# Sums over states by accumulating transfers, C in two banks, and unsplit MLP inputs in a hybrid attention and state-space kernel

## The chip, the cores and the metric

The kernel runs on one core of one Trainium2 chip. A core has five engines with a queue each: TensorE (PE in the profile; its weight loads are PEld), VectorE (DVE), ScalarE (ACT), GpSimd (POOL) and SyncE (SP), which issues most transfers. Sixteen DMA engines carry out the transfers of all queues. Data lie in SBUF, in PSUM (eight banks of 128 x 512 fp32, where PE writes) or in DRAM. The metric is the device time of one execution in microseconds (us); smaller is better.

## The reference

The input x has 4 sequences of 1024 tokens with 128 channels, fp32. Four residual blocks follow one another, each on a LayerNorm of x: attention (16 heads, a window of 32 keys and every 64th key), an MLP, a state-space block, and the same MLP again.

```python
x = x + attn(layernorm(x))
x = x + ffn(layernorm(x))
x = x + mamba(layernorm(x))     # mamba itself adds its input: out = inp + res_scale * ...
x = x + ffn(layernorm(x))

# ffn: three products with weights of +1 and -1, 128 -> 512 -> 512 -> 128, relu between
h = relu(s0 * (concat[x, -x] @ w0)) * 2
h = relu(s1 * (h @ w1)) * 2
return s2 * (h @ w2)

# mamba, E = 256 channels, N = 16 states, per sequence; the core of it:
def step(h, inp):
    dt_t, B_t, C_t, u_t = inp
    dA = exp(dt_t[..., None] * A)
    h = dA * h + (dt_t * u_t)[..., None] * B_t[:, None, :]
    y_t = einsum('ben,bn->be', h, C_t)          # the sum over the 16 states
    return h, y_t
y = (ys + u2 * D_param) * silu(z)
out = y @ W_out
```

## The kernel before

**Stages.** Attention fills the first 232 us. Then comes a stage of MLPs and preparation (232 to 319 us), then the scans of the state-space block (319 to 866 us), with the remaining MLPs of both kinds woven in between, then an end of 35 us.

**Units of the scan.** A half batch is one sequence and one half of its 1024 tokens; there are 8, in the order of `parts_in_order`. A unit is one half batch and one of the 16 states, so there are 128 (`units`). Channels lie on the partitions, in two halves h of 128 (`NH` = 2), tokens run along the free axis (`CH` = 512). For unit i the function `scans` (line 1134; its main loop is at 1211) issues:

- `load_b` (1142): every second unit, a transfer on SP's queue that brings two rows of B, copied to all partitions (`bs`, 512 KB, two buffers);
- `drive` (1150), two units ahead: POOL multiplies `du` by `bs` into `db` (128 x 1024, three buffers);
- `decay` (1158), one unit ahead: ACT takes the exponential into a PSUM bank (`da`, two banks), one h at a time;
- a product on PE that spreads C's row over the partitions into PSUM (`pcc`, one bank);
- two scans on DVE, one for each h, from `da` and `db` into `hs`; the last column is kept in `carry` for the second half of the sequence;
- one product on DVE, `hs` by `pcc`, into `hc` (128 x 1024, six buffers);
- `fold` (1164): POOL adds the `hc` of an even unit to that of the next odd unit, one h in each unit;
- `total` (1171): PE adds the folded pair into `pys` (a PSUM bank for each h), as an fp32 product with the identity. A half batch starts with the product for the term u2 * D (`skip_d`) and has eight such sums for each h;
- `gated` (1183): after the eighth, DVE multiplies the gate by `pys`.

Of the eight PSUM banks, five belong to the scans (`da` 2, `pcc` 1, `pys` 2), three to all other work (`SPARE`, line 1252).

**The order of the work.** Every instruction of the scans goes out through one helper (line 57), and each engine's order is the program's. The other work (MLPs, LayerNorms, preparation of later half batches) is written as generators that yield pieces with estimated costs. `pieces` (1295) is called twice in each unit and issues those that fit by the planner's clock of each engine (`times`, advanced by `spend`, 1256) and by a rate per call (`RATES`, 1278); `evictions` (1282) issues those that empty a PSUM bank. What is left when the last unit is out is issued after it. So the estimates decide at which unit a piece stands in an engine's queue; they do not decide when it runs.

**The MLP** (`mlp`, 739) takes 512 tokens (256 in the last pieces). Its steps: LayerNorm on ACT, four transposes on PE (`ftp`), the copy to SBUF (`fxnT`), the first product (`pf`), relu, the second (`pg`), relu, the third (`pfo`), the residual on DVE. All calls pass `split` as true: inputs of the first two products are held as two single-pass numbers, the rounded value (written by ACT) and the rest (written by DVE, in `empty`, 751), and PE multiplies both parts in turn. In the profile `a` names the MLPs of the first kind, `b` and `c` those of the second; `early`, `late` and `late_batch` (835 to 863) call `mlp`. `in_scan_buffers` (1334) lends buffers of the scan to one MLP that runs before the scans.

Of the kernel before, what the change touches and what calls it, by code (L numbers as in the profile page):

```python
# [43 lines left out]
def hybrid_kernel(ctx: ExitStack, tc: tile.TileContext, x, Wq, Wk, Wv, Wo, ln_g, ln_b, W_in, conv_w,  # L44
# [694 lines left out]
    def mlp(u, tiles, split, pool, lane, own=None, soon=False, hasty=False, stats=None):  # L739
# [39 lines left out]
        xnT = pool.tile([P, 2, cols], kind, name=f"fxnT{u}", tag=f"fxnT{lane}")  # L779
        yield from empty([xnT], [tp], False)  # L780
        for f0 in (0, 2):
            yield fill(1.1 if split else 1.8, 2, ready=(lambda: own or h1_free[0]) if f0 == 0 else None, loose=f0 == 2)
# [9 lines left out]
            for f in range(2):  # L792
                w = wt(w0[:, (f0 + f) * P : (f0 + f + 1) * P])
                for s in range(parts):
                    te.matmul(pf[f], w, xnT[:, s], start=s == 0, stop=s == parts - 1)
# [39 lines left out]
    def early(bp, c, *args):  # L835
        stats = yield from awaited(("a", bp, c))
        tiles = xs[bp][:, 4 * c : 4 * c + 4, :]
        yield from mlp(f"a{bp}_{c}", tiles, True, *args, hasty=bp == 1 and c < HALF, stats=stats)
        fed.add(("a", bp, c))
# [11 lines left out]
    def late_batch(b, f, groups, *args):  # L851
# [5 lines left out]
        yield from mlp(f"c{b}_{f}{groups[0]}", tiles, True, *args, soon=bool(f), stats=stats)  # L857
# [276 lines left out]
    def scans(wide, ready):  # L1134
# [3 lines left out]
        bss, dbs, das, hss = {}, {}, {}, {}  # L1138
# [10 lines left out]

        def drive(i):  # L1150
            if i <= last:
                b, f, n = units[i]
                ready(b, f, NH - 1)
                dbs[i] = m2.tile([P, NH, CH], F32, name=f"db{i}", tag="db", bufs=3)
                bs = bss[i - n % 2][:, n % 2]
                gp.tensor_tensor(dbs[i], mamba_pre[b, f][3], bs.unsqueeze(1).to_broadcast([P, NH, CH]), ALU.mult)
# [7 lines left out]
        def fold(i):  # L1164

            h = i % 2
            k = i - 2 - h
            if 0 <= k <= last:
                gp.tensor_add(hss[k + 1][:, h], hss[k + 1][:, h], hss[k][:, h])

        def total(i):

            h = 1 - i % 2
            k = i - 3 - h
            if not 0 <= k <= last:
                return
            b, f, n = units[k]
            if n == 0:
                py[b, f, h] = wide.tile([P, CH], F32, name=f"pys{b}_{f}{h}", tag=f"pys{h}")
                te.matmul(py[b, f, h], skip_d[:, h], mamba_pre[b, f][1][:, h], start=True, stop=False)  # L1180
            te.matmul(py[b, f, h], ident, hss[k + 1][:, h], start=False, stop=n == N - 2)

        def gated(i):

            h = i % 2
            k = i - 4 - h
            if not 0 <= k <= last:
                return False
            b, f, n = units[k]
            if n == N - 2:  # L1190
                gate = mamba_pre[b, f][0]
                ve.tensor_mul(gate[:, h], gate[:, h], py.pop((b, f, h)))
                if h == NH - 1:
                    fed.add(("g", b, f))
            return n == N - 2
# [12 lines left out]
        for h in range(NH):  # L1208
            decay(0, h)
            done["da", 0, h] = spend("sc", 0.7)  # L1210
        for i, (b, f, n) in enumerate(units):
            now[0] = i
            load_b(i + 3)
            fold(i)
            h0, h1 = i % 2, 1 - i % 2
            done["fold", i] = spend("gp", 1.29, *after(("hc", i - 1 - h0)))
            drive(i + 2)
            done["db", i + 2] = spend("gp", 2.38, *after(("hs", i - 1, 1)))
            pc = wide.tile([P, CH], F32, name=f"pcc{i}", tag="pcc")
            te.matmul(pc, spread[: 6 * N, n, :], mamba_pre[b, f][4], start=True, stop=True)  # L1220
            done["pcc", i] = spend("pe", 0.4, *after(("hc", i - 1)))
            hs = m2.tile([P, NH, CH], F32, name=f"hs{i}", tag="hs")
# [219 lines left out]
```

## Time and profile before

| what | us |
|---|---|
| median of the three runs | 908.13 |
| lowest and highest | 905.29, 908.22 |
| span of the profiled execution (the page gives no other time of it) | 901.9 |
| attention | 0 to 232 |
| MLPs and preparation | 232 to 318.75 |
| scans, first scan to the end of the last `hc` product | 318.75 to 866.45 |
| end | 866.45 to 901.9 |
| busy in the scans: PE, DVE, ACT, POOL | 472.1, 504.6, 409.3, 508.8 |

A group's line in the profile gives the source line (57 for nearly all, the helper), the engine, the operation, output <- inputs with shapes, and the count; then the busy time in us and the mean of one in ns; then the idle time of the engine just before these instructions and what ended it. A line of waits gives who waited for whom, the time in total, how often, and the longest. A line of the timeline gives start, duration, engine, operation and how many instructions it merges; one fp32 product of PE appears as two. In the busy table by stretches each engine's column is us busy, with the number of its instructions in brackets; the last columns are PE's granted clock, the mean busy share of the 16 DMA engines and the rate that they moved.

### The profile page before, as it was taken

How to read it: one execution, taken by the hardware profiler on the slowest of the kernel's cores; microseconds unless marked ns; L12 is line 12 of the kernel's file. 1: busy time of each engine (PE TensorE's matmuls, PEld its weight loads, DVE VectorE, ACT ScalarE, POOL GpSimd, SP SyncE). 2: the span in 40 equal slices, each digit the busy share in tenths (PEclk: the TensorE clock that was granted, in tenths of full speed). 3: DMA queues.
4: the chain of work that ended last, by engine and by line, in shares of the span. 5: the costliest groups of instructions: out<-in, count | busy, mean ns of one | idle time of the engine just before them, and what ended most of it. 6: DMA issues, size and time to landing. Idle time of an engine off the chain costs nothing. (4 is left out here: it accounts for less than half of the span.)

```text
span 901.9 us, 16464 instructions
## 1 busy us (share of the span) xinstructions
PE 756.2 (84%) x6226; PEld 463.5 (51%) x6226; DVE 754.3 (84%) x994; ACT 607.1 (67%) x1358; POOL 727.0 (81%) x566
## 2 busy tenths in 40 slices
PE   5897779866798978879899888779889989989777
PEld 2454546544577642335456554335455545656457
DVE  6799999999533289798899999989988898999962
ACT  4776648744445488888787888888777766654423
POOL 6799958998322199999999999999988987997930
PEclk9899989987789997789999999899989999999899
DMA  4733123330100111121221211212111121221100
GB/s 127 131 73 70 43 44 69 72 65 2 43 7 1 49 53 66 67 74 48 70 69 51 70 48 70 72 47 72 70 72 59 53 78 59 70 82 58 60 7 19
DMA packets 47152, 53.18 MB, mean 59 GB/s; under 512 B 4808, under 2 KB 38384, under 8 KB 47072
## 3 DMA queue, kind: packets, MB, share of 16 engines
q1 hardware_dynamic: 45904, 51.59, 20.4%
q8 instruction: 49, 0.80, 0.4%
q0 software_dynamic: 608, 0.27, 0.2%
q10 hardware_dynamic: 560, 0.26, 0.1%
q14 instruction: 31, 0.25, 0.1%
HBM read 45.82 MB, written 4.46 MB: 56 GB/s over the span
## 5 line engine op out<-in xcount | busy, mean ns | idle before, releaser
L57 POOL TENSOR_TENSOR db<-du,bs 128x1024 f32<-128x1024 f32 x128 | 302.4, 2363 | 0.1
L57 ACT ACTIVATE da<-dt,a_t 128x512 f32<-128x512 f32 x256 | 175.5, 688 | 123.2 <-DVE hs L57 122.7
L57 POOL TENSOR_TENSOR hc<-hc,hc 128x512 f32<-128x512 f32 x128 | 162.8, 1272 | 29.1 <-DVE hc L57 28.8
L57 DVE TENSOR_TENSOR hc<-hs,pcc 128x1024 f32<-128x1024 f32 x128 | 155.9, 1218 | 23.7 <-PE pcc L57 15.4
L57 DVE TENSOR_TENSOR_SCAN hs<-da,db 128x512 f32<-128x512 f32 x128 | 149.4, 1207 | 20.7 <-ACT da L57 15.5
L57 DVE TENSOR_TENSOR_SCAN hs<-da,carry,db 128x512 f32<-128x512 f32 x128 | 156.9, 1266 | 1.2 <-ACT da L57 1.2
L57 PE MATMUL pys<-hc,ident 128*128 128x512 f32 x256 | 145.3, 651 | 6.1 <-POOL hc L57 6.0
L57 POOL TENSOR_TENSOR prodv<-vS,E 128x128 f32<-128x128 f32 (+14 forms) x30 | 69.3, 2311 | 11.5 <-ACT E L57 11.3
L57 PEld LDWEIGHTS pys<-hc,ident 128*128 128x128 f32 x256 | 49.8, 208 | 53.7 <-issue 28.1
L57 PE MATMUL pcc<-bc,spread 96*128 96x512 bf16 x128 | 51.5, 402 | 29.6 <-DVE hc L57 28.7
L57 PE MATMUL pga<-h1a,w 128*128 128x512 f32 x256 | 70.5, 425 | 2.7 <-DVE h1a L57 1.9
L57 POOL TENSOR_TENSOR prod<-kv,qs 128x128 f32<-128x128 f32 (+14 forms) x30 | 71.1, 2369 | 0.8 <-DVE or L57 0.8
L57 ACT ACT_TABLE_LOAD x48 | 61.6, 1283 | 3.5 <-issue 2.6
L57 PE MATMUL pc<-mxnT,w_conv 128*128 128x512 f32 x128 | 61.5, 606 | 2.0 <-ACT gate L57 2.0
L57 PEld LDWEIGHTS pga<-h1a,w 128*128 128x128 f32 x256 | 49.3, 195 | 25.5 <-issue 4.7
L57 ACT ACTIVATE E<-S 128x512 f32<-128x512 f32 (+15 forms) x62 | 26.5, 473 | 39.7 <-DVE S L57 39.5
L57 PE MATMUL ps<-kx,qT 64*32 64x256 f32 x1008 | 43.5, 416 | 5.8 <-DVE S L57 5.0
L57 POOL TENSOR_TENSOR du<-dt,u 128x512 f32<-128x512 f32 x16 | 20.4, 1275 | 30.5 <-ACT dt L57 30.5
L57 ACT COPY ep<-pt 128x512 f32<-128x512 f32 x32 | 18.7, 586 | 35.8 <-DVE eo L57 35.5
L57 PEld LDWEIGHTS pc<-mxnT,w_conv 128*128 128x128 f32 x128 | 24.6, 194 | 33.9 <-issue 26.7
L57 PE MATMUL pgb<-h1b,w 128*128 128x512 f32 x128 | 37.5, 439 | 4.8 <-DVE h1b L57 3.3
L57 PE MATMUL pgc<-h1c,w 128*128 128x256 f32 (+1 forms) x192 | 37.2, 346 | 0.0
(244 smaller groups left out, 1637.5 us busy)
## 6 DMA issues: line engine op xcount, KB each, us to landing
bs<-bd SPq DMA_DIRECT2D x64, 512.0 KB
vr<-vd SPq DMA_DIRECT2D x32, 256.0 KB
vd<-kv SPq DMA_DIRECT2D x8, 256.0 KB
x<-in_L_attn_a_x_dram SPq DMA_DIRECT2D x15, 128.0 KB
kx<-kT SPq DMA_DIRECT2D x104, 16.0 KB
out_dram<-x SPq DMA_DIRECT2D x8, 128.0 KB
taps<-in_L_attn_b_conv_w_dram SPq DMA_DIRECT2D x1, 512.0 KB
out_dram<-ox SPq DMA_DIRECT2D x2, 256.0 KB
```

The costliest lines, as they stand in the source:

```text
L57: ins = getattr(self.engine, name)(*args, **kwargs)
```

## The change

1. The product `hs` by `pcc` is written back over the unit's `db`. Two units share one tile (1 MB, `[P, 2, NH, CH]`). The tile of a half batch's first pair (`acc`, two buffers) collects: for pairs two to seven POOL issues a transfer that adds the pair's tile to it (`gather`). The tiles of pairs two to eight come from three buffers (`pr`). The folds on POOL are gone.
2. PE adds the eighth pair, and then the collecting tile, in the first units of the next half batch: for each h the `skip_d` product and four sums, h after h in one bank (`pys`). After the last unit they follow at once, with h = 1 in a bank of `pcc`.
3. `pcc` has two banks, and the spread of unit i + 1 is issued in unit i.
4. The MLP's input `fxnT` is one fp32 copy by ACT, multiplied by PE in one fp32 product. It stays split in the first two MLPs (buffers lent from `gate`) and in the last two half MLPs.
5. The planner's figures follow (`spend`, `fill`).

```diff
--- before.py
+++ after.py
@@ -736,7 +736,7 @@
 
     h1_free = [True]
 
-    def mlp(u, tiles, split, pool, lane, own=None, soon=False, hasty=False, stats=None):
+    def mlp(u, tiles, split, pool, lane, own=None, soon=False, hasty=False, stats=None, halves=None):
 
 
 
@@ -776,10 +776,15 @@
         tp = bank(f"ftp{u}")[:, :cols]
         for i in range(nt):
             te.transpose(tp[:, i * P : (i + 1) * P], xn[:, i, :], ident)
-        xnT = pool.tile([P, 2, cols], kind, name=f"fxnT{u}", tag=f"fxnT{lane}")
-        yield from empty([xnT], [tp], False)
+        if halves:
+            xnT = halves(u)
+            yield from empty([xnT], [tp], False)
+        else:
+            xnT = pool.tile([P, 1, cols], F32, name=f"fxnT{u}", tag=f"fxnT{lane}")
+            yield evict(sc=0.57)
+            sc.copy(xnT[:, 0], tp)
         for f0 in (0, 2):
-            yield fill(1.1 if split else 1.8, 2, ready=(lambda: own or h1_free[0]) if f0 == 0 else None, loose=f0 == 2)
+            yield fill(1.1 if halves else 2.1, 2, ready=(lambda: own or h1_free[0]) if f0 == 0 else None, loose=f0 == 2)
             if f0 == 0:
                 if own:
                     h1 = own(u)
@@ -790,9 +795,11 @@
                 h2 = pool.tile([P, 4, cols], F32, name=f"h2{u}", tag=f"h2{lane}")
             pf = [bank(f"pf{u}_{f0 + f}")[:, :cols] for f in range(2)]
             for f in range(2):
-                w = wt(w0[:, (f0 + f) * P : (f0 + f + 1) * P])
-                for s in range(parts):
-                    te.matmul(pf[f], w, xnT[:, s], start=s == 0, stop=s == parts - 1)
+                w = w0[:, (f0 + f) * P : (f0 + f + 1) * P]
+                w = w if halves else w.bitcast(F32)
+                n = xnT.shape[1]
+                for s in range(n):
+                    te.matmul(pf[f], w, xnT[:, s], start=s == 0, stop=s == n - 1)
             yield from empty(h1[f0 : f0 + 2], pf, True)
         for f0 in (0, 2):
             yield fill(2.05 if split else 1.8, 2, loose=f0 == 2)
@@ -835,7 +842,8 @@
     def early(bp, c, *args):
         stats = yield from awaited(("a", bp, c))
         tiles = xs[bp][:, 4 * c : 4 * c + 4, :]
-        yield from mlp(f"a{bp}_{c}", tiles, True, *args, hasty=bp == 1 and c < HALF, stats=stats)
+        first = first_in if bp == 0 and c < HALF else None
+        yield from mlp(f"a{bp}_{c}", tiles, True, *args, hasty=bp == 1 and c < HALF, stats=stats, halves=first)
         fed.add(("a", bp, c))
 
     def late(bp, c, *args):
@@ -848,13 +856,13 @@
                 tiles[b2 * R : (b2 + 1) * R],
             )
 
-    def late_batch(b, f, groups, *args):
+    def late_batch(b, f, groups, *args, **kwargs):
 
         stats = yield from awaited(("c", b, f))
         g = slice(groups[0], groups[-1] + 1)
         tiles = own_x[b, f][:, g]
         stats = stats[:, :, g]
-        yield from mlp(f"c{b}_{f}{groups[0]}", tiles, True, *args, soon=bool(f), stats=stats)
+        yield from mlp(f"c{b}_{f}{groups[0]}", tiles, True, *args, soon=bool(f), stats=stats, **kwargs)
         to = out[b, f * (T // 2) : (f + 1) * (T // 2)].rearrange("(g p) c -> p g c", p=P)
         nc.sync.dma_start(to[:, g], tiles)
         fed.add(("b", b, f, groups[0]))
@@ -1135,7 +1143,7 @@
 
 
 
-        bss, dbs, das, hss = {}, {}, {}, {}
+        bss, prs, das, pcs = {}, {}, {}, {}
         py = {}
         last = len(units) - 1
 
@@ -1147,13 +1155,18 @@
                 bss[i] = m2.tile([P, 2, CH], F32, name=f"bs{i}", tag="bs", bufs=2)
                 nc.sync.dma_start(bss[i], mamba_pre[b, f][5][n : n + 2, :].partition_broadcast(P))
 
+        def pair(i):
+            return prs[i - i % 2][:, i % 2]
+
         def drive(i):
             if i <= last:
                 b, f, n = units[i]
                 ready(b, f, NH - 1)
-                dbs[i] = m2.tile([P, NH, CH], F32, name=f"db{i}", tag="db", bufs=3)
+                if n % 2 == 0:
+                    tag, bufs = ("pr", 3) if n else ("acc", 2)
+                    prs[i] = m2.tile([P, 2, NH, CH], F32, name=f"pr{i}", tag=tag, bufs=bufs)
                 bs = bss[i - n % 2][:, n % 2]
-                gp.tensor_tensor(dbs[i], mamba_pre[b, f][3], bs.unsqueeze(1).to_broadcast([P, NH, CH]), ALU.mult)
+                gp.tensor_tensor(pair(i), mamba_pre[b, f][3], bs.unsqueeze(1).to_broadcast([P, NH, CH]), ALU.mult)
 
         def decay(i, h):
             if i <= last:
@@ -1161,38 +1174,42 @@
                 das[i, h] = wide.tile([P, CH], F32, name=f"da{i}_{h}", tag="da", bufs=2)
                 sc.activation(das[i, h], mamba_pre[b, f][2][:, h], AF.Exp, scale=a_t[:, h, n : n + 1])
 
-        def fold(i):
-
-            h = i % 2
-            k = i - 2 - h
-            if 0 <= k <= last:
-                gp.tensor_add(hss[k + 1][:, h], hss[k + 1][:, h], hss[k][:, h])
-
-        def total(i):
-
-            h = 1 - i % 2
-            k = i - 3 - h
-            if not 0 <= k <= last:
-                return
-            b, f, n = units[k]
-            if n == 0:
-                py[b, f, h] = wide.tile([P, CH], F32, name=f"pys{b}_{f}{h}", tag=f"pys{h}")
+        def spread_c(i):
+            if i <= last:
+                b, f, n = units[i]
+                pcs[i] = wide.tile([P, CH], F32, name=f"pcc{i}", tag="pcc", bufs=2)
+                te.matmul(pcs[i], spread[: 6 * N, n, :], mamba_pre[b, f][4], start=True, stop=True)
+
+        def gather(i):
+
+            k = i - 2
+            if not 0 <= k <= last or k % 2 or units[k][2] in (0, N - 2):
+                return False
+            gp.dma_start(prs[k - units[k][2]], prs[k], accum_op=ALU.add)
+            return True
+
+        def total(e, h, step, tag="pys"):
+
+            b, f, n = units[e]
+            if step == 0:
+                py[b, f, h] = wide.tile([P, CH], F32, name=f"pys{b}_{f}{h}", tag=tag, bufs=2 if tag == "pcc" else 1)
                 te.matmul(py[b, f, h], skip_d[:, h], mamba_pre[b, f][1][:, h], start=True, stop=False)
-            te.matmul(py[b, f, h], ident, hss[k + 1][:, h], start=False, stop=n == N - 2)
-
-        def gated(i):
-
-            h = i % 2
-            k = i - 4 - h
-            if not 0 <= k <= last:
-                return False
-            b, f, n = units[k]
-            if n == N - 2:
-                gate = mamba_pre[b, f][0]
-                ve.tensor_mul(gate[:, h], gate[:, h], py.pop((b, f, h)))
-                if h == NH - 1:
-                    fed.add(("g", b, f))
-            return n == N - 2
+            t = prs[e - n if step else e - 1]
+            for j in range(2):
+                te.matmul(py[b, f, h], ident, t[:, j, h], start=False, stop=step == 1 and j == 1)
+
+        def gated(e, h):
+
+            b, f, n = units[e]
+            gate = mamba_pre[b, f][0]
+            ve.tensor_mul(gate[:, h], gate[:, h], py.pop((b, f, h)))
+            if h == NH - 1:
+                fed.add(("g", b, f))
+
+        def ended(i):
+
+            e = i - (i + 1) % N
+            return (e, i - e) if e >= 0 else (0, N)
 
 
         done = {}
@@ -1208,19 +1225,17 @@
         for h in range(NH):
             decay(0, h)
             done["da", 0, h] = spend("sc", 0.7)
+        spread_c(0)
+        done["pcc", 0] = spend("pe", 0.4)
         for i, (b, f, n) in enumerate(units):
             now[0] = i
             load_b(i + 3)
-            fold(i)
-            h0, h1 = i % 2, 1 - i % 2
-            done["fold", i] = spend("gp", 1.29, *after(("hc", i - 1 - h0)))
             drive(i + 2)
             done["db", i + 2] = spend("gp", 2.38, *after(("hs", i - 1, 1)))
-            pc = wide.tile([P, CH], F32, name=f"pcc{i}", tag="pcc")
-            te.matmul(pc, spread[: 6 * N, n, :], mamba_pre[b, f][4], start=True, stop=True)
-            done["pcc", i] = spend("pe", 0.4, *after(("hc", i - 1)))
-            hs = m2.tile([P, NH, CH], F32, name=f"hs{i}", tag="hs")
-            db = dbs.pop(i)
+            if gather(i):
+                spend("gp", 0.95, *after(("hc", i - 1)))
+            hs = m2.tile([P, NH, CH], F32, name=f"hs{i}", tag="hs", bufs=2)
+            db = pair(i)
             for h in range(NH):
                 first = carry[b % 2][:, h, n : n + 1] if f else 0.0
                 ve.tensor_tensor_scan(hs[:, h], das.pop((i, h)), db[:, h], first, ALU.mult, ALU.add)
@@ -1234,19 +1249,24 @@
                 sc.copy(carry[b % 2][:, :, n : n + 1], hs[:, :, CH - 1 :])
             decay(i + 1, 1)
             done["da", i + 1, 1] = spend("sc", 0.67 if f else 0.86, *after(("hs", i, 1)))
-            if gated(i):
+            e, past = ended(i)
+            if past in (3, 5):
+                gated(e, past == 5)
                 spend("ve", 0.68, *after(("sum", i - 1)))
-            hss[i] = m2.tile([P, NH, CH], F32, name=f"hc{i}", tag="hc", bufs=6)
-            ve.tensor_tensor(hss[i], hs, pc.unsqueeze(1).to_broadcast([P, NH, CH]), ALU.mult)
+            ve.tensor_tensor(db, hs, pcs.pop(i).unsqueeze(1).to_broadcast([P, NH, CH]), ALU.mult)
             done["hc", i] = spend("ve", 1.205, *after(("pcc", i)))
-            total(i)
-            done["sum", i] = spend("pe", 1.0, *after(("fold", i - 1)))
+            spread_c(i + 1)
+            done["pcc", i + 1] = spend("pe", 0.4, *after(("hc", i - 1)))
+            if 1 <= past <= 4:
+                total(e, past > 2, 1 - past % 2)
+                done["sum", i] = spend("pe", 3.2 if past % 2 else 2.2)
             t = times["ve"]
             pieces(t + 2.2)
-        for i in range(last + 1, last + 6):
-            fold(i)
-            gated(i)
-            total(i)
+        for h in range(NH):
+            for step in range(2):
+                total(last, h, step, "pcc" if h else "pys")
+        for h in range(NH):
+            gated(last, h)
 
 
     SPARE = 3
@@ -1333,7 +1353,12 @@
 
     def in_scan_buffers(u):
 
-        return [m2.tile([P, 2, CH], F32R, name=f"h1{u}_{f}", tag="hc", bufs=6) for f in range(4)]
+        pairs = [m2.tile([P, 2, 2, CH], F32R, name=f"h1{u}_{f}", tag="pr", bufs=3) for f in range(2)]
+        return [t[:, f] for t in pairs for f in range(2)]
+
+    def first_in(u):
+
+        return m2.tile([P, 2, CH], F32R, name=f"fxnT{u}", tag="gate", bufs=4)
 
     first_half = range(HALF)
     second_half = range(HALF, CT)
@@ -1411,7 +1436,12 @@
             def own(u):
                 return [pool.tile([P, 2, 2 * C], F32R, name=f"h1{u}_{f}", tag=f"h1{u}_{f}") for f in range(4)]
 
-            weave(*(Work(late_batch(B - 1, 1, range(2 * k, 2 * k + 2), pool, k, own)) for k in range(2)))
+            def halves(u):
+                return pool.tile([P, 2, 2 * C], F32R, name=f"fxnT{u}", tag=f"fxnT{u}")
+
+            weave(*(
+                Work(late_batch(B - 1, 1, range(2 * k, 2 * k + 2), pool, k, own, halves=halves)) for k in range(2)
+            ))
 
 
 # ---- launch: one core ----
```

## The prediction

> **What bounds the kernel now.** I read the busy table by slices first, then busy time in the stretch of the scans, then VectorE's waits in that stretch, and last the end of the timeline. The change lies in the scans (first scan 318.75 us, last `hc` product ends 866.45 us: 547.7 us for 128 units, 4.28 us each).
>
> ```profile
> core 0: us, PE busy (x) PEld busy (x) DVE busy (x) ACT busy (x) POOL busy (x), PEclk, DMA share, GB/s
> 318.70:866.50 547.80, 472.17 (x1710) 265.15 (x1708) 504.58 (x493) 409.39 (x869) 508.81 (x378) 0.92 0.19 63
> ```
>
> Two engines are nearly full: POOL 93%, DVE 92%. PE has 76 us free, ACT 138 us; the DMA engines are busy 19%.
>
> ```profile
> DVE hs L57 <- ACT da L57: 16.7, 15, 8.3
> DVE hc L57 <- PE pcc L57: 15.4, 16, 2.9
> DVE x L57 <- PE pfob L57: 3.2, 3, 2.0
> DVE hs L57 <- POOL db L57: 3.0, 3, 1.6
> DVE hs L57 <- POOL hc L57: 2.1, 1, 2.1
> ```
>
> DVE idles 43.2 us in the stretch. POOL, though full, ends only 5.1 us of it; 15.4 us are waits for C's spread (`pcc`), which has one bank, so that its matmul waits for the product before. The 8.3 us wait is the start, before the first scan.
>
> ```profile
> L57 POOL TENSOR_TENSOR db<-du,bs 128x1024 f32<-128x1024 f32 x128 | 302.4, 2363 | 0.1
> L57 POOL TENSOR_TENSOR hc<-hc,hc 128x512 f32<-128x512 f32 x128 | 162.8, 1272 | 29.1 <-DVE hc L57 28.8
> ```
>
> So most that the scans can give is DVE's idle time and the work taken from DVE, not POOL's 162.8 us.
>
> **The change, part by part.**
>
> *Folds leave POOL.* 128 adds (162.8 us) go; 48 accumulating transfers of 1 MB come (six of the eight pairs of a half batch, eight half batches). One issue on POOL: the issues of `w_xp` took 0.70 to 0.71 us, and the code's own planner books 0.95; I take 0.95, so 46 us. POOL falls to about 392 us of work. What DVE gains at once are the 5.1 us of POOL waits.
>
> *The new wait.* The products now lie in three pair tiles, and POOL's `db` for a pair writes the tile that the transfer three pairs back reads. In POOL's order (`db` first half, transfer of the previous pair, `db` second half) this makes a loop: transfer of pair p lands, then `db` of pair p+3 (2.36), then the issue for pair p+1. With S the time from issue to landing, the loop takes S + 2.36 a pair, against two units of DVE, 2T. T will be about 517/128 = 4.04 us (below). A scan starves only when the lag has used up POOL's lead, 2T - 2.36 = 5.7 us plus one 2.36; about five waits of a half batch are chained, so scans stall for 5 x (S - 7.75) us in each of 8 half batches: 40 x (S - 7.75). Behind a waiting `db` on POOL stand the next issue, the second `db`, the LayerNorm scalings and `du`; ACT and DVE wait for those.
>
> S is in no row of before. Rows near it:
>
> ```profile
> DMA to landing us min/median/max: 2.0/2.2/3.6
> ```
> ```profile
> DMA packets 144, 0.52 MB, mean 175 GB/s; under 512 B 16, under 2 KB 16, under 8 KB 144
> q1 hardware_dynamic: 144, 0.52, 45.7%
> ```
>
> The first is `w_xp` (32 KB, POOL's queue): 2.2 us fixed. The second is one `bs` load, alone in the window 403 to 406 us: 45.7% of 3 us is 1.37 us of all 16 engines for 0.52 MB, so 2.75 us for one pass over 1 MB. Lower end: one pass, 2.2 + 2.75 = 4.95. Upper end: source read, destination read and write one after another, 2.2 + 8.25, and a `bs` load of 1.37 in between (there is one a pair), 11.8. The `bs` row is a whole copy in which read and write overlap; accumulating adds one read to it. I therefore take one and a half to two passes, about 7 us, below 7.75: no stall. Two full passes give 7.7, at the threshold; with the `bs` load in the way, 9.1 and a stall of 40 x 1.35 = 54 us. The ends are 0 and 40 x 4.05 = 162 us.
>
> The Trainium skill speaks here, in "Collectives: The Full Stack", section "The bandwidth ceiling: the fold count and why AG ≠ RS ≠ AR": a reducing transfer emits two source reads on one ring, so it runs at half a copy's rate. Doubling the row above by that rule gives the 7.7; the page's own 31 GB/s per engine, halved, would give 64 KB in 4.2 us (an estimate from its figure), hence 6.4 and no stall. No transfer of before reduces, so the trace can't choose.
>
> *Two banks for C.* The spread for unit i+1 is issued in unit i, a unit ahead: 15.4 us of waits go, unless PE is late by a whole unit. The third bank comes from `pys`, whose two halves now follow each other in one bank.
>
> *MLP inputs whole.* In the scans DVE loses `fxnT` subtractions: 4 + 4 of 0.67, 2 of 0.67, 2 of 0.41, 7.5 us. PE pays: two single-pass products (0.27 each; eight `pga` took 2.22) become one fp32 product of 1.02, +0.47, four an MLP, 13 MLPs: +25 us over the kernel. The sums over states lose 64 fp32 products (128 + 16 before, 80 after), 65 us at 1.02. In the scans PE stays below DVE.
>
> *Scans summed.* Some DVE work (3 us of it) moves behind the last scan: DVE 504.6 - 7.5 - 3 = 494. Idle 43.2 - 15.4 - 5.1 = 22.7; the waits for ACT and for evictions stay. Together 517, against 547.8: -31.
>
> *Before the scans.* The MLPs of the third and fourth tile group now have eight fp32 products (+3.8 us of PE), and the last two stand ahead of the convolution; the first scan stands behind the addition of the fourth MLP's output, in the program's order. The subtractions (PE waited 2.4 us around them) go. Bounds 0 and +6; I take +3.
>
> *The end.* Before, from the last product to the last MLP's first transpose:
>
> ```profile
> 867.84 2.35 PE L57 MATMUL pys<-hc,ident 128*128 128x512 f32 x4 [1.52 <-POOL hc L57]
> 870.02 1.95 PE L57 MATMUL pfoc<-w,h2c 128*128 128x128 f32 x16
> ...
> 876.58 4.03 PE L57 MATMUL pgc<-h1c,w 128*128 128x256 f32 x32
> ...
> 884.05 0.66 PE L57 MATMUL ftpc<-ident,fxnc 128*128 128x128 f32 x4 [0.58 <-DVE ox L57]
> ```
>
> That is 17.6 us, PE nearly full. In the changed program's order PE has after the last product: 8 sums (8.2; skip and one state can run ahead), a whole `pfoc` of 16 products (3.8), two times four fp32 `pfc` at 256 columns (2.0 each), `pmo` (4.1), two `pgc` groups of 4.03, two half `pfoc` (1.95, and 2.5 with its wait), two transposes (0.7): 33.3 us. The planner books fewer side pieces per unit, so one more half MLP and more are left over. +16; bounds +8 (PE fills gaps before) and +20. The last of the six transfers was issued two units (7.4 us) before the last product, so its landing costs under 1 us.
>
> *Sum.* -31 + 3 + 16 = -12. On the span, 901.9 - 12 = 890; the median (908.1) lies 6.2 above the profiled span, and runs go from 905.3 to 908.2. Forecast 896, 1.3% faster. About 0.3% is what a measurement of this kernel can tell from no change: 905.4 to 910.9 counts as the same.
>
> **Rivals.**
>
> *The transfers set the pace (slower).* One mechanism: POOL's `db` waits for the landing, from S = 7.75 on; the gain is gone at 12/40 above that, S = 8.05. For it: two reads and the `bs` loads on the same engines give 9.1. Against it: the engines idle 81% of the time, and 4.95 is possible. At 9.1: 896 + 54 = 950; at 8.5: 926.
>
> *A standoff.* S near 8, or PE reaches the spread late behind bursts (three sums of 1.02 in a row, then MLP pieces) so that `pcc` waits stay: 15 of the 31 us are lost, 908. Against it: the spread has a unit of room.
>
> *Backlog hidden.* The left-over pieces at the end run in PE's free time, +8 instead of +16, and the start costs nothing: 896 - 8 - 3 = 885. Against it: the order on PE puts them behind the sums.
>
> **How the numbers follow.** Forecast 0.45 (its own range 887 to 905), backlog hidden 0.08 (879 to 887), standoff 0.08 (905 to 911), transfers set the pace 0.39 (911 upwards, to 1058 at S = 11.8). Faster 0.52, same 0.09, slower 0.39, a little of the forecast's upper edge counted as same. The range of eight in ten leaves out about 5 in a hundred below 884 and 14 above 950.
>
> **What would show it.** Right: no fold on POOL, POOL's `db` waiting for transfers by little, DVE's idle time for `pcc` near nothing, scans of about 517 us, 48 issues of 1024 KB that land in under 7.75 us; the time from the last product to the end some 16 us longer than 35.4. Wrong: S above 8, seen as POOL idle before `db` and DVE's `hs` waiting for POOL; scans above 530; or PE the one whom DVE waits for.

## The result and the profile after

The changed kernel takes **936.73 us** (median of four runs, 935.6 to 937.08) against 906.71 us (904.09 to 908.22) for the kernel before, measured beside it: a ratio of 1.034 with a 95% interval of 1.032 to 1.037. It is 3.4% slower. The forecast was 896 us, 1.3% faster. The time lies within the stated range, on the side of the rival "the transfers set the pace".

First the busy table of the changed kernel by stretches (preparation, scans, end; columns as for the kernel before):

```profile
232.00:328.20 96.20, 86.31 (x624) 62.18 (x625) 31.10 (x67) 47.47 (x98) 27.74 (x34) 0.93 0.10 29
328.20:879.00 550.80, 429.90 (x1457) 236.29 (x1455) 497.00 (x475) 402.91 (x851) 392.68 (x297) 0.86 0.66 151
879.00:934.60 55.60, 46.43 (x312) 38.21 (x312) 12.12 (x35) 17.35 (x47) 1.58 (x4) 0.97 0.12 29
```

All three stretches grew: preparation by 9.45 us, scans by 3.1, end by 20.15. Together that is the difference of the spans (934.6 against 901.9), 32.7 us. The medians differ by 30.0. The work of the scans is what was forecast: VectorE 497.0 us busy (494 forecast), POOL 392.7 (392). But VectorE idles 53.8 us there, not 22.7. Its waits in the scans:

```profile
DVE hs L57 <- POOL pr L57: 20.3, 15, 3.2
DVE hs L57 <- ACT da L57: 17.8, 18, 3.0
DVE x L57 <- PE pmo L57: 3.5, 1, 3.5
```

The waits for `pcc` (15.4 us before) are gone. In their place VectorE waits for POOL, although POOL is now only 71% busy. The groups on POOL, the queue and the issues on the page say what POOL waits for:

```profile
q0 software_dynamic: 7520, 50.60, 29.4%
...
L57 POOL TENSOR_TENSOR pr<-du,bs 128x1024 f32<-128x1024 f32 x128 | 313.4, 2482 | 124.0 <-DMA pr<-pr 116.3
...
L57 POOL DMA_DIRECT2D pr<-pr x48 | 42.9, 893 | 13.3 <-DVE hs L57 7.0
...
pr<-pr POOLq DMA_DIRECT2D x48, 1024.0 KB, 7.9
```

POOL's products are held up 116 us by transfers that have not landed; the median time from issue to landing is 7.9 us. POOL's timeline shows the loop itself, here in the second half batch:

```profile
482.60 0.90 POOL L57 DMA_DIRECT2D pr<-pr  x1
483.28 2.62 POOL L57 TENSOR_TENSOR pr<-du,bs 128x1024 f32<-128x1024 f32 x1
490.61 2.34 POOL L57 TENSOR_TENSOR pr<-du,bs 128x1024 f32<-128x1024 f32 x1 [4.70 <-DMA pr<-pr]
492.89 0.87 POOL L57 DMA_DIRECT2D pr<-pr  x1
...
510.33 2.36 POOL L57 TENSOR_TENSOR pr<-du,bs 128x1024 f32<-128x1024 f32 x1 [2.40 <-DMA pr<-pr]
512.63 0.92 POOL L57 DMA_DIRECT2D pr<-pr  x1
513.32 2.62 POOL L57 TENSOR_TENSOR pr<-du,bs 128x1024 f32<-128x1024 f32 x1
...
520.68 2.37 POOL L57 TENSOR_TENSOR pr<-du,bs 128x1024 f32<-128x1024 f32 x1 [4.54 <-DMA pr<-pr]
523.00 0.87 POOL L57 DMA_DIRECT2D pr<-pr  x1
```

An issue at 512.63; the product that needs its landing can start at 520.68, 8.05 us later; behind it stands the next issue, at 523.00. One turn takes 10.4 us, while two units take 8.2 where no transfer holds them up (522.7 us for 128 units, first experiment below).

The order does a second thing. POOL's second product of the turn runs from 513.32 to 515.94, and its end frees the `bs` buffer that the next load of B takes. SP's timeline has that load 0.03 us behind it:

```profile
515.97 0.32 SPq L1156 DMA_DIRECT2D bs<-bd  x1
```

So the load of B runs beside the accumulating transfer of the same turn. It did so in 34 of the 48 turns, 3.3 to 3.6 us after the transfer's issue, and these transfers landed after 7.8 to 8.9 us (median 7.9); the six that met no load of B landed after 6.9 to 7.1 us.

The last issue, at 876.51, comes late in the same way, and TensorE's timeline at the end shows it:

```profile
879.07 1.12 PE L57 MATMUL pys<-pr,ident 128*128 128x512 f32 x2 [0.53 <-DVE pr L57]
883.52 3.51 PE L57 MATMUL pys<-pr,ident 128*128 128x512 f32 x4 [3.33 <-DMA pr<-pr]
886.87 1.02 PE L57 MATMUL pys<-u,skip_d 128*128 128x512 f32 x2
887.73 3.60 PE L57 MATMUL pys<-pr,ident 128*128 128x512 f32 x8
```

### The profile page after: what moved, and what is told of

It reads as the page before. It is cut to its first block, busy times and chain, and to the rows that moved or that the text cites. A ratio compares the mean times of both kernels' runs of the same rounds, so it can differ in the third digit from the quotient of the medians.

```text
span 934.6 us, 16094 instructions
## 1 busy us (share of the span) xinstructions
PE 739.4 (79%) x6098; PEld 450.0 (48%) x6098; DVE 749.0 (80%) x980; ACT 608.8 (65%) x1358; POOL 614.2 (66%) x486
## 5 line engine op out<-in xcount | busy, mean ns | idle before, releaser
L57 POOL TENSOR_TENSOR pr<-du,bs 128x1024 f32<-128x1024 f32 x128 | 313.4, 2482 | 124.0 <-DMA pr<-pr 116.3
L57 DVE TENSOR_TENSOR_SCAN hs<-da,pr 128x512 f32<-128x512 f32 x128 | 149.7, 1209 | 29.9 <-POOL pr L57 15.9
L57 DVE TENSOR_TENSOR pr<-hs,pcc 128x1024 f32<-128x1024 f32 x128 | 156.0, 1219 | 9.8 <-DVE hs L57 0.5
L57 DVE TENSOR_TENSOR_SCAN hs<-da,carry,pr 128x512 f32<-128x512 f32 x128 | 157.0, 1268 | 8.3 <-POOL pr L57 4.4
L57 PE MATMUL pcc<-bc,spread 96*128 96x512 bf16 x128 | 55.0, 433 | 22.7 <-DVE pr L57 21.9
L57 PEld LDWEIGHTS pga<-h1a,w 128*128 128x128 f32 x256 | 50.6, 201 | 22.1 <-DVE h1a L57 3.1
L57 POOL DMA_DIRECT2D pr<-pr x48 | 42.9, 893 | 13.3 <-DVE hs L57 7.0
L57 PE MATMUL pgb<-h1b,w 128*128 128x512 f32 x128 | 42.2, 483 | 7.5 <-DVE h1b L57 6.3
L57 POOL TENSOR_TENSOR du<-dt,u 128x512 f32<-128x512 f32 x16 | 23.3, 1464 | 32.3 <-ACT dt L57 32.3
L57 PE MATMUL pfa<-fxnTa,w 128*128 128x512 f32 x64 | 33.0, 642 | 12.4 <-DVE h1a L57 5.4
L57 ACT COPY ep<-pt 128x512 f32<-128x512 f32 x32 | 18.8, 586 | 36.5 <-DVE eo L57 36.2
L57 PEld LDWEIGHTS pgb<-h1b,w 128*128 128x128 f32 x128 | 28.7, 228 | 20.7 <-DVE h1b L57 8.1
```

Source lines behind the costliest of these rows:

```text
L57: ins = getattr(self.engine, name)(*args, **kwargs)
```

## The experiments

The times of all kernels in one place. The start is counted from PE's first transpose of `mxn`, since attention before it ends at different times from one profiled execution to the next (first transpose at 280.4 to 285.1 us). Stages are from the one profiled execution, times are medians; the run without transfers was timed once. The kernel before had medians of 906.0 to 906.6 beside these runs.

| kernel | time | start | scans | end |
|---|---|---|---|---|
| before | 906.7 | 36.5 | 547.7 | 35.5 |
| changed | 936.7 | 45.0 | 550.8 | 55.6 |
| no transfers | 903.5 | 43.4 | 522.7 | 50.5 |
| transfer first | 906.4 | 43.4 | 524.9 | 51.2 |
| half transfers | 904.3 | 45.0 | 524.5 | 51.2 |
| turns kept | 927.3 | 39.0 | 547.7 | 54.4 |
| rate 3.3 | 929.2 | 43.4 | 548.1 | 50.6 |
| before, inputs whole | 923.0 | 43.4 | 543.0 | 49.7 |
| transfer first, one bank | 926.8 | 43.4 | 543.5 | 52.3 |
| transfer first, inputs split | 906.0 | 37.8 | 538.0 | 48.3 |
| the same, rate 3.1 | 907.3 | 37.8 | 542.3 | 37.6 |
| transfer first, turns kept | 901.8 | 39.0 | 527.7 | 51.2 |
| the same, rate 3.3 | 900.3 | 39.0 | 534.1 | 44.4 |

### Without the transfers

```diff
-            gp.dma_start(prs[k - units[k][2]], prs[k], accum_op=ALU.add)
-            return True
+            return False
```

> The changed kernel without its 48 accumulating transfers; what they add to the sums over states (pairs two to seven of each half batch) is left out. In the changed kernel the scans took 550.8 us (first scan 328.2, last product ends 879.0). Theory A: POOL's waits for the transfers (120 us, of which DVE inherits 20 us at once and the waits for da as a follow-up) are what ate the gain that I forecast in the scans. Then POOL waits for no transfer, DVE waits for POOL under 5 us, and the scans take 515 to 530 us; the end, 55.6 us, loses about 3 us of waiting for the last transfer. Rival B: the scans are held by something else (PE's queue, ACT's exponentials, the order of the side pieces); then they stay at 540 us or more without transfers. The start stays at 328 us by both.

903.49 us. VectorE's waits for POOL are gone and the scans take 522.7 us:

```profile
328.50:851.20 522.70, 423.82 (x1458) 231.53 (x1456) 495.43 (x475) 405.36 (x855) 350.68 (x251) 0.88 0.19 66
```

So the transfers cost the scans 28 us. The run also shows that the start and the end stay long without them. Even with transfers that cost nothing the change would have won next to nothing: this one execution lies within the range of the kernel before beside it (902.2 to 909.1, median 906.0).

### The same transfers, issued before the product

```diff
-            drive(i + 2)
-            done["db", i + 2] = spend("gp", 2.38, *after(("hs", i - 1, 1)))
             if gather(i):
                 spend("gp", 0.95, *after(("hc", i - 1)))
+            drive(i + 2)
+            done["db", i + 2] = spend("gp", 2.38, *after(("hs", i - 1, 1)))
```

> The changed kernel with each transfer issued ahead of the db of its step instead of behind it. The loop of the changed kernel is landing (7.9 us median) plus db (2.4 us) per pair, 10.3 us, against 8.6 us for two units as measured; with the issue ahead of db the loop is the landing alone, 7.9 us. Theory A: POOL's waits for transfers fall from 120 us to under 50, DVE's waits for POOL from 20 us to under 6, scans from 551 to about 530, the whole by 15 to 22 us to 915 to 922. Rival B (not the loop but the transfers' traffic or other waits hold the scans): within 4 us of 936.7. Rival C: db now waits behind a transfer that itself waits for the product, so DVE's waits for POOL stay or grow: 937 to 945.

906.37 us, ratio 0.9997 (0.998 to 1.002): 30 us came back from two lines changing places, more than expected. POOL's waits and its timeline over the same stretch:

```profile
POOL pr L57 <- DVE pr L57: 70.1, 30, 8.4
...
POOL pr L57 <- DMA pr<-pr: 12.9, 6, 3.1
```
```profile
507.61 0.90 POOL L57 DMA_DIRECT2D pr<-pr  x1 [1.76 <-DVE pr L57]
508.26 2.63 POOL L57 TENSOR_TENSOR pr<-du,bs 128x1024 f32<-128x1024 f32 x1
510.58 0.51 POOL L57 TENSOR_SCALAR st_z<-mv_z 128x4 f32<-128x4 f32 x1
510.78 2.63 POOL L57 TENSOR_TENSOR pr<-du,bs 128x1024 f32<-128x1024 f32 x1
517.06 0.90 POOL L57 DMA_DIRECT2D pr<-pr  x1 [3.64 <-DVE pr L57]
```

Now an issue mostly waits for VectorE's product of its own pair, which means that POOL is ahead of VectorE. The six waits for a landing are waits of an issue too, for the transfer before it, which adds to the same collecting tile:

```profile
435.59 0.90 POOL L57 DMA_DIRECT2D pr<-pr  x1 [2.74 <-DMA pr<-pr]
```

No product stands between a landing and the next issue any more. The shortest turn took 7.5 us, less than the 8.2 us of two units. The load of B no longer falls into the landing either: it starts some 2 us before the issue or more than 5 us after it in most turns, and the median landing is 7.0 us instead of 7.9. The same 48 MB move, the DMA share is as high (0.67 against 0.66), and the scans are within 2.2 us of those without any transfer. The traffic itself costs next to nothing; the order on one queue cost 26 us. How much of that is the product in the loop and how much the longer landing, no run tells apart.

### Half the bytes in the old order

```diff
-            gp.dma_start(prs[k - units[k][2]], prs[k], accum_op=ALU.add)
+            gp.dma_start(prs[k - units[k][2]][:, 0], prs[k][:, 0], accum_op=ALU.add)
```

> The changed kernel in its own order (product first, transfer second), but each transfer carries only the even state of its pair, 512 KB instead of 1 MB; it leaves out the odd states of the pairs 2 to 7 from the sums. If the loop (landing, then the next product, then the next issue) is what cost the scans, then a shorter landing breaks it without any change of order: landing about 2.2 + 2.85 = 5.1 us (4.5 to 5.7), loop 7.4 us against 8.1 us of VectorE work a pair, POOL waits for transfers under 15 us, scans 522 to 528 us, total 907 to 914 us. If most of the 7.9 us is a fixed cost, landing stays at 6.5 us or more and the scans at 535 us or more, total above 920 us. If only the place of the issue matters and not how long the transfer takes, the scans stay near 551 us and the total near 937 us.

904.28 us (ratio 0.997, 0.9955 to 0.999), a little below the 907 to 914 expected; scans 524.5 us, as expected. The page's issues, POOL's waits and the queue:

```profile
pr<-pr POOLq DMA_DIRECT2D x48, 512.0 KB, 4.6
```
```profile
POOL pr L57 <- DMA pr<-pr: 3.5, 2, 2.1
```
```profile
q0 software_dynamic: 7520, 25.44, 15.0%
```

The kernel leaves out half of what the transfers should add. At 4.6 us the old order does no harm. Both ways of breaking the loop, a shorter landing and another order, give the same scans. More than half of the landing goes with the bytes: 15.0% of 901.6 us is 135 us, 2.8 us of all 16 engines for each 512 KB, and 5.7 us for each 1 MB in the changed kernel.

### The start: turns kept

While two MLPs and the preparation run in turns, one `yield` is one turn. The whole input has one `yield` fewer for an MLP than the split one, so the MLPs get ahead in the turns. At the end of the turns a lane that holds PSUM banks must finish its piece before the scans get theirs (lines 1397 to 1399 of the changed kernel); in the changed kernel the fourth MLP's last product and its addition come out ahead of the first scan. ScalarE's timeline, changed kernel:

```profile
321.38 0.60 ACT L57 ACTIVATE h2a<-pga 128x512 f32<-128x512 f32 x1 [1.80 <-PE pga L57]
326.07 1.28 ACT L57 ACT_TABLE_LOAD   x1 [4.09 <-DVE x L57]
327.36 1.30 ACT L57 ACTIVATE da<-dt,a_t 128x512 f32<-128x512 f32 x2
```

```diff
             sc.copy(xnT[:, 0], tp)
+            yield evict()
```

> The changed kernel with one empty step put back into the MLP, where the subtraction for the split input used to be. Ahead of the scans the pieces are taken in turns, and a lane that holds PSUM banks when the turns end must finish its step before the banks of the scans are handed out; the changed kernel thus runs the fourth MLP's last product and addition before the first scan (328.2 us against 318.75 before). Theory D: the missing step shifted the turns; with it back the first scan starts at 321 to 324 us, and the whole is 4 to 7 us shorter (930 to 933). Rival E: the start is late because the fp32 products are longer and stand ahead of the convolution; then it stays at 326 us or later and the whole within 3 us of 936.7.

927.26 us (ratio 1.023, 1.020 to 1.026), 9.5 us less than the changed kernel and more than the 4 to 7 expected. The same place in this kernel:

```profile
321.05 0.60 ACT L57 ACTIVATE h2a<-pga 128x512 f32<-128x512 f32 x1 [1.27 <-PE pga L57]
321.66 1.28 ACT L57 ACT_TABLE_LOAD   x1
322.96 1.30 ACT L57 ACTIVATE da<-dt,a_t 128x512 f32<-128x512 f32 x2
```

The 4.09 us wait is gone, and the start is 39.0 us instead of 43.4 to 45.0. The rest of the gain lies in the scans (3.1 us) and the end (1.2 us).

### The end: a higher rate for TensorE's pieces

```diff
-    RATES = {"pe": 2.9, "ve": 1.2, "sc": 2.4, "gp": 1.2}
+    RATES = {"pe": 3.3, "ve": 1.2, "sc": 2.4, "gp": 1.2}
```

> The changed kernel with the planner's rate of side work on PE raised from 2.9 to 3.3 us a unit, so that more MLP pieces are issued among the scans; on PE 16 products of pgc at 512 columns, 16 of pfoc and 4 of pfc fewer stand behind the last spread of C. Theory F: the end (55.6 us against 35.4 before) is longer by the pieces left over; it falls to 46 to 49 us, the scans lengthen by under 3 us, the whole falls by 5 to 9 us to 928 to 932. Rival G: the pieces do not fit among the scans either; the scans lengthen by as much as the end shortens and the whole stays within 3 us of 936.7.

929.24 us (ratio 1.024, 1.020 to 1.028): 7.5 us less, as expected. The end is 5 us shorter, but at 50.6 us it stays above the 46 to 49 expected, and the scans are 2.7 us shorter. The edits taken together, below, show that the gain does not come again once the transfers no longer hold up the scans.

### One part alone: MLP inputs whole

The kernel before, with the hunks of the change on `mlp`, `early`, `late_batch`, `first_in` and the last `weave`, and none of the others; its core:

```diff
-        xnT = pool.tile([P, 2, cols], kind, name=f"fxnT{u}", tag=f"fxnT{lane}")
-        yield from empty([xnT], [tp], False)
+        if halves:
+            xnT = halves(u)
+            yield from empty([xnT], [tp], False)
+        else:
+            xnT = pool.tile([P, 1, cols], F32, name=f"fxnT{u}", tag=f"fxnT{lane}")
+            yield evict(sc=0.57)
+            sc.copy(xnT[:, 0], tp)
...
```

> The kernel before with one part of the change alone: the inputs of the MLPs kept whole (as in the changed kernel, the first two and the last two in halves); folds and C as before. Theory: the longer start comes from this part (first scan at 327 to 329 us instead of 318.8), and half or more of the longer end (48 more products of pgc, 16 of pfoc and 4 of the transposes behind the last spread, about 8 us more); the scans gain at most the 7.5 us of subtractions and, with POOL at 93%, rather 0 to 4 us. Together 906 + 9.5 + 8 - 3 = 920 us (914 to 926). Rival: start and end come from the sums over states, and this part alone gives 899 to 908 us.

922.99 us, ratio 1.018 (1.015 to 1.021), as the theory had it. The scans, and VectorE's first wait in them:

```profile
328.20:871.20 543.00, 467.10 (x1588) 247.08 (x1588) 495.29 (x475) 403.64 (x851) 503.86 (x375) 0.94 0.18 63
```
```profile
DVE hc L57 <- PE pcc L57: 22.2, 17, 5.3
```

VectorE loses 9.3 us of work, but the scans only 4.7, since its waits for `pcc` grow from 15.4 to 22.2. The start is 6.9 us longer, the end 14.2. This part brought in no transfer and no new sum, and by itself costs 1.8%.

### One part undone: C in one bank

The kernel with the transfer first, and

```diff
-                pcs[i] = wide.tile([P, CH], F32, name=f"pcc{i}", tag="pcc", bufs=2)
+                pcs[i] = wide.tile([P, CH], F32, name=f"pcc{i}", tag="pcc", bufs=1)
...
-                py[b, f, h] = wide.tile([P, CH], F32, name=f"pys{b}_{f}{h}", tag=tag, bufs=2 if tag == "pcc" else 1)
+                py[b, f, h] = wide.tile([P, CH], F32, name=f"pys{b}_{f}{h}", tag=tag, bufs=1)
```

> The kernel with the transfer issued first, but C's spread in one bank instead of two (this part of the change undone, the rest kept). If the second bank bought what the waits of before promised (15.4 us of VectorE waits for pcc), the time rises from 906.4 to about 921 us (917 to 925), and VectorE waits for pcc come back with 12 to 18 us. Rival: the waits for the spread were there only because the engine also waited for the folds and PE was fuller; now PE gets to the spread in time or DVE spends the time waiting elsewhere: 906 to 911 us.

926.8 us against 906.4, scans 18.6 us longer (in the fastest of the five executions, 921.4 us, which is the one profiled). The loss is a little above the range expected, and the place is another: VectorE waits for `pcc` 1.2 us in all. It is TensorE that waits. Its wait for VectorE's product with two banks, and then with one:

```profile
PE pcc L57 <- DVE pr L57: 23.6, 17, 3.2
```
```profile
PE pcc L57 <- DVE pr L57: 106.6, 67, 4.3
```

The spread stands at the head of TensorE's queue, and everything behind it gets late: VectorE's waits of `gate` for the sums grow from 2.2 to 9.8 us, and waits for other work of TensorE and ScalarE take up more of the rest. In this program the spread is issued right behind the product and ahead of the sums, so it is not quite the one bank of before.

### The other part alone: inputs split, transfer first

```diff
+            high = pool.tile([P, cols], F32R, name=f"fxnT{u}", tag=f"fxnT{lane}")
+            low = fx.tile([P, nt, C], F32R, name=f"fxnL{u}", tag=f"fxn{lane}", bufs=1)
+            xnT = Halves(high, low.rearrange("p i c -> p (i c)"))
+        yield from empty([xnT], [tp], False)
-            xnT = pool.tile([P, 1, cols], F32, name=f"fxnT{u}", tag=f"fxnT{lane}")
-            yield evict(sc=0.57)
-            sc.copy(xnT[:, 0], tp)
...
-            yield fill(1.1 if halves else 2.1, 2, ready=(lambda: own or h1_free[0]) if f0 == 0 else None, loose=f0 == 2)
+            yield fill(1.1, 2, ready=(lambda: own or h1_free[0]) if f0 == 0 else None, loose=f0 == 2)
...
-        first = first_in if bp == 0 and c < HALF else None
+        first = None
```

> The changed kernel with the transfer first and without the part on the MLP inputs: they stay split in two halves as before (the low half lies in the buffer of the normalized input, which is free by then). So the sums over states and the two banks are alone here, as the inputs kept whole were alone in the run before. If that part is what made start and end longer (there: start +9.5, scans -4.7, end +14.3 us), then the first scan is back at 318 to 320 us, the scans are 525 to 533 us (at most the 7.5 us of subtractions come back), the end is 40 to 47 us, and the time is about 889 us (885 to 897). Rival: the sums over states make start or end longer too: first scan after 323 us or end above 49 us, time 898 us or more.

906.0 us, ratio 0.9987 (0.997 to 1.0003): the theory's sum fell, though its start came true when counted from the first transpose. (The profiled execution, 910.9 us, was the longest of the twelve, so its stages are some 5 us long together.) The start is back to 37.8 us, the end only to 48.3, and the scans went from 524.9 to 538.0: 8 us of subtractions on VectorE, 5 us more idle time. So the parts don't add. With the folds, whole inputs cost 16.3 us; with the transfers issued first they cost nothing in the median. In the end, each part alone leaves 13 to 14 us more than before, and both together 16.

The same with a rate of 3.1:

```diff
-    RATES = {"pe": 2.9, "ve": 1.2, "sc": 2.4, "gp": 1.2}
+    RATES = {"pe": 3.1, "ve": 1.2, "sc": 2.4, "gp": 1.2}
```

> The same with TensorE's rate for side pieces 3.1 instead of 2.9: behind the last spread 32 products of pgc fewer (0.134 us each, 4.3 us) and two transposes. If the pieces find free time on TensorE in the scans, the end is 4 us shorter and the time 4 us below the kernel with split inputs at 2.9 (881 to 893). Rival: as in the kernel with three edits, more pieces in the scans come back as waits of VectorE, the scans are 4 to 9 us longer, and nothing is won.

907.34 us (ratio 0.9998, 0.998 to 1.002). In the profiled executions the end is 10.7 us shorter and nearly that of before, and the scans are 4.3 longer. In the median nothing is won, as the rival had it. The two profiled executions lie 4.9 us above and 2.9 us below the medians of their kernels, so these two figures don't explain the medians.

### The edits together

Transfer first, turns kept and a rate of 3.3, the three edits as above.

> The three edits that each won time alone, together: transfer issued ahead of the product of du and B, the turns before the scans kept as they were, TensorE's rate for side pieces 3.3 instead of 2.9. If the three work in different places (the transfers' loop in the scans, the wait for banks before them, the pieces left over behind them), their gains add: from 906.4 us (transfer first alone) take 9.5 us for the turns (as measured alone: 936.7 to 927.3) and about 5 us for the rate (16 fewer products of pgc, 16 of pfoc and 4 of pfc behind the last spread: 2.0 + 1.95 + 1.03 us): 892 us, 888 to 895, first scan at 323 to 324 us, scans of 521 to 526 us, end 45 to 48 us. Rival: with the loop gone VectorE and TensorE share the scans more tightly, and pieces that run earlier or at a higher rate come back as waits of the scans: scans 530 us or more, total 897 us or more.

900.33 us, ratio 0.994 (0.991 to 0.996): faster than both kernels, but by 6 us, not by 14. To tell which edit cost the scans their 9 us, the rate was set back to 2.9:

> The changed kernel with two edits, transfer issued first and turns kept, TensorE's rate for side pieces left at 2.9. The three edits together gave 900.3 us, with scans of 534 us where transfer first alone had 524.9. If the higher rate cost the scans those 9 us, this kernel has the first scan at 323 to 326 us, scans of 523 to 527 us, an end of 50 to 52 us, and a time of 899 to 904 us. If the kept turns cost them (MLP work that the start no longer does runs in the scans), scans are 530 us or more and the time is 905 to 911 us.

901.78 us, ratio 0.9945 (0.992 to 0.997). The scans and the end, with the rate of 3.3 and then with 2.9:

```profile
323.70:857.75 534.05, 436.07 (x1540) 244.44 (x1539) 497.71 (x481) 407.25 (x864) 399.50 (x300) 0.89 0.66 159
857.75:902.10 44.35, 38.83 (x263) 31.79 (x261) 9.74 (x29) 11.88 (x34) 1.26 (x2) 1.00 0.04 13
```
```profile
320.70:848.35 527.65, 425.03 (x1488) 239.32 (x1487) 495.72 (x476) 404.04 (x855) 399.61 (x300) 0.88 0.66 161
848.35:899.50 51.15, 45.42 (x315) 37.93 (x313) 12.09 (x34) 15.49 (x43) 1.26 (x2) 0.99 0.06 17
```

The rate moves 6.8 us from the end into the scans, which grow by 6.4. In the changed kernel the same edit shortened the end by 5 us and the scans did not grow (548.1 against 550.8): there VectorE waited for POOL meanwhile, so that TensorE's extra pieces had time. That reason is argued from the stages, not shown by a run of its own. The first scan came 3 us earlier than expected only because attention ended earlier in that execution; counted from the first transpose the start is the same 39.0. The kept turns are worth 4.4 us in the start and give 2.8 of them back in the scans.

Not tried: a fourth pair buffer in the changed kernel's own order, and that order with the load of B moved out of the landing.

## Why the prediction was wrong, point by point

**The new wait: the step that failed.** The prediction named the loop, its place and the waits behind it, and put the price at zero. Two terms of that step were mis-sized. First S. A transfer that met no load of B landed after 6.9 to 7.1 us, so "about 7" was right for such a one. The prediction knew that one `bs` load comes in each pair, and left it out of the value that it took; in 34 of 48 turns the load fell into the landing, and the median was 7.9 us. Second the threshold: 7.75 doesn't follow from the step's own numbers. The lead of 5.7 + 2.36 = 8.1 us, spread over five chained waits, is 1.6 us a wait; 2 x 4.04 - 2.36 + 1.6 gives 7.3 (7.75 results if only four waits share it). With 40 x (S - 7.75), S = 7.9 gives 6 us; with 40 x (S - 7.3) it gives 24. Measured were 26 us against the same transfers in the other order and 28 us against none. So the form of the term fits and its price was off twice: the forecast had S 0.75 us below the threshold, where S lay 0.6 us above the corrected one. By the corrected term S = 7.0 would still have cost nothing (an estimate; no run has the changed order with such landings).

The Trainium skill's rule that a reducing transfer reads twice ("Collectives: The Full Stack", section "The bandwidth ceiling: the fold count and why AG ≠ RS ≠ AR") agrees with this case's engine times: 2.8 us for 512 KB against 1.37 us for the `bs` load of that size, though that load comes from DRAM. The two estimates of S that the prediction drew from that page, 7.7 and 6.4 us, lie on either side of the undisturbed 7.0, and neither has the load of B in it.

**The rest of the scans.** VectorE's work was right (494 forecast, 497 measured), POOL's too (392 and 393), an issue took 0.89 us (0.95 taken), and the `pcc` waits went. Without the loop the scans are 524.9 us instead of 517: VectorE idles 29.3 us, not 22.7. The waits for `da`, assumed to stay (8.4 us without the one before the first scan), were 13.9, and the waits of `gate` for the sums grew from 0.7 to 2.2 us. "The waits for ACT and for evictions stay" was the weak sentence.

**Two banks for C.** The waits of 15.4 us went, as forecast. Undoing the second bank in the kernel with the transfer first cost 18.6 us in the scans; there it was TensorE's queue that stood still, and VectorE's own wait for `pcc` was 1.2 us.

**Before the scans.** Forecast +3 with bounds up to +6, measured +8.5 and, in most executions with whole inputs, +6.9. The products and subtractions were counted. That the addition of the fourth MLP stands ahead of the first scan was said too; that one `yield` fewer brings this about, and what the wait costs, was not. 4.5 us belong to that, shown by the kept turns.

**The end.** +16 forecast, +20.2 measured, of which 3.3 us are TensorE's wait for the last landing, which was put at under 1 us, since the last issue was taken to come two units ahead. POOL's queue, late by the loop, issued it at 876.51. With the transfer first the end is +15.7, as forecast.

**What it adds up to.** With the loop taken out, the working would have given -12; measured is -0.3 (906.4 against 906.7). Scans +8 against the forecast and start +4 make up the difference. Of the rivals, "the transfers set the pace" is what happened, nearer to its lower end; at S = 7.9 its own formula gives 902 us, so it had the mechanism and not the price. "Backlog hidden" did not: the pieces stayed behind the sums. "A standoff" had S near 8, which came, but priced it at 15 us; its other half did not come, as no `pcc` waits remained.

## What to carry to other kernels

When an engine's queue holds both the issue of a transfer and the work that waits for the previous landing, put the issue first if the landing alone is shorter than a turn: then that work is out of the loop, and two lines were worth 30 us here. Look also at what else the order starts: here the work behind the issue released a load that fell into the landing. When a forecast hangs on a threshold, work the threshold out again from its own terms and compare the margin with the uncertainty of the duration; a margin of 0.75 us on a landing bounded only between 4.95 and 11.8 us is no margin. A planner's rate moves work between a stage and its end; it wins only what the stage spends waiting.

## What the runs showed of the hardware

An accumulating transfer from SBUF to SBUF took 2.8 us of all 16 engines for 512 KB and 5.2 to 5.7 us for 1 MB, and landed in 4.6 and in 7.0 to 7.9 us (medians). In the changed kernel the 1 MB landed in 6.9 to 7.1 us with no load of B in between and in 7.8 to 8.9 us with a load of 512 KB issued 3.3 to 3.6 us after it. With the transfer first, where few loads fall into the landing, the median was 7.0 us. This is read from the transfers of these kernels; no run moved the load alone.

POOL's product of 128 x 1024 takes 2.36 us, but in the changed kernel 2.62 to 2.70 right behind an issue on the same engine. With the transfer first most products that start within 5 us of an issue are as long (2.6 us), the second of a pair too. Its mean was 2.364 us without transfers, 2.482 in the changed kernel and 2.588 with the transfer first.

The granted clock of TensorE in the scans was 0.92 before and 0.94 with whole inputs alone, and 0.84 to 0.89 in every kernel with the new sums, at 0.88 also without any transfer. So it isn't the transfers. TensorE has 35 to 54 us less to do there; whether that lowers the clock, no run tells apart.
